# Reordering the last graph's projections: means directly behind the last v products, two q products two tiles later, and q gathers that wait for one tile

## The chip, the cores and the metric

The kernel runs on one core of a Trainium2 chip. The metric is the device time of one execution in microseconds (us), as the median of several runs of the same program. A single core runs here, so its time is the time of the kernel.

## The reference

Thirty-two graphs of 512 nodes with 512 features each share one sparse 0/1 adjacency matrix (density 0.0078, some 4 neighbours for each node). Each graph goes through two layers, everything in float32:

```python
# layer 0: masked attention, 8 heads of 64
h = relu(layernorm(x))
q, k, v = h @ Wq + bq, h @ Wk + bk, h @ Wv + bv      # split in heads
scores = q @ k.T / 8 + (1 - adj) * -1e9
x = x + softmax(scores) @ v @ Wo + bo
# layer 1: graph attention
h = relu(layernorm(x)) @ W
e = leaky_relu(h @ a1 [:, None] + h @ a2 [None, :]) * adj
x = x + elu(softmax(e) @ h + beta * h)
```

A node with no neighbour attends to all nodes alike in layer 0, so its result is the mean of all v. The kernel keeps these means as extra rows of the table of v.

## The kernel before

**Tiles and stages.** A graph has T = 4 tiles of 128 nodes; B = 32 graphs give 128 tiles. The nodes are permuted once so that each tile's edges fit 4 groups of 128 gathered rows. Two stages alternate:

- `stage_a(b)` makes the projections of graph b. For two tiles at a time, `turned_state` fetches x, normalises it and transposes it into `hT`; `keys_and_values` makes k and v of both tiles with seven half products (L872, a Strassen-like scheme) and stores them in the table `tab`; `queries` makes q (L42 with `wq,hT`), adds the bias on DVE (L804), copies in a column of the older graph (L807) and stores q in the table `qtab`. At the end come the means: `means` (L932) sums the v of the four tiles on TensorE, ACT scales them (L939), and four small SP stores (L943) put them into `tab`. All plain stores of these tables are issued by SP (`put`, L911).
- `stage_b(b)` does the edge work for each tile of graph b, and layer 1 for the same tile of graph b - LAG, with LAG = 2. POOL issues four kv gathers (L960; 128 rows with k and v of graph b and the layer-1 state of graph b - 2) and four q gathers (L983) for each tile. DVE multiplies and sums q times k (L1028, L1031), ACT takes the exponential and weighs v (L1037, L1042), and DVE makes the layer-1 weights of the edges (L1170). Then TensorE forms the edge sums (L1015, one bank `pd` for layer 1 and `px` for layer 0), transposes (L741) and runs the dense products with `wo` and `w` (L42). POOL also raises the variance to the power -0.5 in each norm (L761), fetches x for the residual (L774), and stores the output rows (L779, after L1238 on DVE).

The loop is `for b in range(B + LAG)`: stage_a(b + 1) while b + 1 < B, then stage_b(b). So graph 31's projections run beside the edge work of graphs 29 and 30, and no projections run after them. For the last two values of b only layer 1 is left; its gathers read smaller tables, `th`.

**Order.** The engines' programs are written out by a planner (`Plan.order`) before the launch. Every operation has an engine, an estimated duration, and a key, which is a due time in the planner's own units: tile n has the base `100 + 20 n`, S = 20 is one tile, and the projections of graph b start AHEAD = 6 tiles before its edge work. Among operations that can start at once on an engine, the one with the lowest key goes first; on TensorE a change of the matmul's form (128 rows or groups of 32) adds STAY = 1.0 to the key. An operation that is ready is never held back for its key alone: when nothing with a lower key can start within 0.2 us, it goes. Each engine then executes its list strictly in that order and waits where an input isn't there.

**Keys around the change** (in tiles; graph 31 begins at tile 124): the q products of its tiles 2 and 3 have 121.28 and 121.9, the last half product of v 121.74, the means 122 and 0.02 us. The edge sums of tile n have n + 1, the transposes n + 1.48, the product with `wo` n + 1.72, the layer-1 product n + 1.88. The gathers of tile n have n - 0.85 and n - 0.84.

**Buffers.** The gathered kv rows lie in a ring of 5 (`kv`), the gathered q rows in a ring of 2 (`qe`); each buffer holds two of the four groups of a tile. A kv buffer comes free with the edge sums of its tile.

**Waits.** A kv gather waits for everything that is written to `tab` of its graph: k, v and layer-1 state of four tiles and the means' rows. A q gather waits for everything that is written to `qtab` of its graph, thus for the q of all four tiles, though it reads rows of one tile only (and one zero row).

**Fillers.** `run_on` puts matmuls with no use for the result in front of some products of the last tiles: two matmuls behind the edge sums of the last five tiles of the edge work (L1078), and six in front of the edge sums of the first two tiles of graph 31 (L1183). They are always executed; the profile shows them as L42 with `wq` alone.

Of the kernel before, what the change touches and what calls it, by code (L numbers as in the profile page):

```python
# [64 lines left out]
class Plan:  # L65
# [14 lines left out]
    def buf(self, tag, name=""):  # L80
        return Buf(tag, name)
# [137 lines left out]
def kernel(  # L219
# [24 lines left out]
    B, N, D = x.shape  # L244
    T = N // P
# [20 lines left out]
    def wtile(shape, name, dt=F32):  # L266
        return work.tile(shape, dt, name=name, tag=name)

    def ring(n, shape, name):
        return [wtile(shape, f"{name}{i}") for i in range(n)]  # L270
# [3 lines left out]
        "hT": ring(3, [P, C, P], "hT"),  # L274
        "S": ring(3, [P, C // 2, P], "S"),
        "oT": ring(1, [P, C, P], "oT"),
# [37 lines left out]
    idx, qidx = wtile([P, T, NG], "idx", I32), wtile([P, T, NG], "qidx", I32)  # L314
# [11 lines left out]
    C_ = {n: buf(None, n) for n in (  # L326
        "wq", "wk", "wv", "wo", "w1", "rows", "c_row", "wa", "OH", "nzE", "idx", "qidx", "fin",
        "rmax", "dmax", "bad", "cap", "flag", "perm", "posi", "t1", "t2", "t3", "t4",
    )}
# [46 lines left out]
    def edges():  # L376
# [10 lines left out]
        def flat(b):  # L387
            return b.ap.rearrange("p a b -> p (a b)") if b.tag == "kv" else b.ap

        def f3(b, n, m):  # L390
            return flat(b)[:, : n * m].rearrange("p (n m) -> p n m", n=n)
# [194 lines left out]
        en = buf("w", "en")  # L586
        S = T * NG

        def enx():
            return flat(en)[:, : S * (MAXDEG + 3)].rearrange("p (t g m) -> p t g m", t=T, g=NG)  # L590

# [16 lines left out]
        def index():  # L608
            e = flat(en)[:, : S * (MAXDEG + 3)].rearrange("p (s m) -> p s m", s=S)
            m = flat(sc)  # L610
            kk, fi, no = m[:, 0:S], m[:, 32 : 32 + S], m[:, 64 : 64 + S]
            eq = f3(val, S, MAXDEG)

# [96 lines left out]


    S = 20.0
    AHEAD = 6

    def base(n):
        return 100.0 + n * S
# [18 lines left out]
    def dense(p, lhs, w):  # L735
        for c in range(C):
            product(nc, p, lhs[:, c, :], w[:, c, :], start=c == 0, stop=c == C - 1)
# [61 lines left out]
    def queries(b, t, key, hT):  # L799
        s = st[b]  # L800
        p, q = buf("D", "pq"), buf("q", f"q{b}_{t}")
        o = op("PE", 3.43, key, lambda: dense(p.ap, hT.ap, wq), r=[hT, C_["wq"]], w=[p])
        plan.reserve(o, q)
        op("DVE", 0.7, key, lambda: nc.vector.tensor_tensor(q.ap[:, 0:D], p.ap, bq_r, op=ALU.add), r=[p, C_["rows"]], w=[(q, "q")])  # L804
        if b >= LAG:
            s1 = st[b - LAG]["s1"]
            op("DVE", 0.1, key, lambda: nc.vector.tensor_copy(q.ap[:, D : D + 1], s1.ap[:, t : t + 1]),  # L807
               r=[(s1, t)], w=[(q, "s1")])
        put(b, lambda: s["qtab"].ap, t, lambda: q.ap, key, q, [(s["qtab"], t)])
# [98 lines left out]
    def put(b, dst, t, src, key, part, w):  # L908

        if b:  # L910
            op("SP", 0.1, key, lambda: nc.sync.dma_start(dst()[ts(t, P)], src()), r=[part], w=w, dma=P * D * 4)  # L911
        else:
            op("POOL", 1.3, key, lambda: nc.gpsimd.indirect_dma_start(
                dst()[:N], bass.IndirectOffsetOnAxis(ap=posi[:, t : t + 1], axis=0), src(), None,
                bounds_check=N - 1, oob_is_err=False), r=[part, C_["posi"]], w=w, dma=P * D * 4)

    def stage_a(b):
        s = st[b]
        s["qtab"] = buf("qtab", f"qtab{b}")
        mv, vs = buf("mv0", f"mv0_{b}"), []  # L920
        for t in range(0, T, 2):
            keys = [base(T * b + u - AHEAD) if b else 2.0 + 0.4 * S * u for u in (t, t + 1)]
            hT = [turned_state(b, u, key, mv) for u, key in zip((t, t + 1), keys)]
            vs += keys_and_values(b, t, keys[1], *hT) if b else plain_keys_and_values(t, keys, hT)
            for u in range(2):
                queries(b, t + u, keys[1] + (0.28, 0.9)[u] * S if b else keys[u] + 0.56 * S, hT[u])
        key = base(T * b + T - AHEAD) + 0.02 if b else keys[1] + S
        pv, vm = buf("D", "pvm"), buf("v", f"vm{b}")

        def means():  # L930
            for t in range(T):
                nc.tensor.matmul(  # L932
                    pv.ap[ts(t, G), :].rearrange("p (h f) -> p h f", f=HD), one32, vs[t][1]()[:, :, 0:HD],
                    start=True, stop=True,
                )

        o = op("PE", 1.0, key, means, r=[b for b, _ in vs], w=[pv], form=4)
        plan.reserve(o, vm)
        op("ACT", 0.62, key, lambda: nc.scalar.activation(  # L939
            vm.ap[:, :, 0:HD], pv.ap.rearrange("p (h f) -> p h f", f=HD), AF.Copy, scale=float(G) / P), r=[pv], w=[vm])  # L940
        tab, cols = place(b, VO, H * VW)
        for t in range(DUMMY):
            op("SP", 0.1, key, lambda t=t: nc.sync.dma_start(  # L943
                cols()[N + t : N + t + 1],
                vm.ap[G * t : G * t + 1].rearrange("p h f -> p (h f)")),
               r=[vm], w=[(tab, ("m", t))], dma=2080)

    def stage_b(b):

        s = st[b] if b < B else None  # L950
        old = st[b - LAG] if b >= LAG else None
        if old is not None:
            old["dn"] = buf("dn", f"dn{b}")
        if s is not None:
            s["x1"], s["hx"] = [None] * T, [None] * T
            s["mv1"], s["s1"] = buf("mv1", f"mv1_{b}"), buf("s1", f"s1_{b}")
            s["rd"] = buf("rd", f"rd{b}")

        def gather(dst, tab, t, g):
            nc.gpsimd.indirect_dma_start(  # L960
                dst, None, tab.ap, bass.IndirectOffsetOnAxis(ap=idx[:, t, g : g + 1], axis=0),
                bounds_check=N + DUMMY - 1, oob_is_err=False,
            )

        for t in range(T):
            kb = base(T * b + t)
            slots = [buf("kv", f"kv{b}_{t}_{i}") for i in range(2 if s is not None else 1)]
            slots += slots[len(slots) - 1 :] * (2 - len(slots))
            held = [{n: buf(None, n) for n in ("K", "V", "H")} for _ in range(2)]
            of = {KO: "KVH", VO: "VH", HO: "H"}  # L970
            for g in range(NG):
                for tab, c0, c1 in st[b]["tab"]:
                    op("POOL", 1.3, kb - 0.85 * S + 0.1 * g, lambda slots=slots, g=g, t=t, tab=tab, c0=c0, c1=c1: gather(
                        row(slots, g, c0, c1 - c0), tab, t, g),
                       r=[tab, C_["idx"]],
                       w=[(slots[g // 2], (g, c0)), *((held[g // 2][n], (g % 2, "row")) for n in of[c0])],
                       dma=P * (c1 - c0) * 4)
            if s is not None:
                qs = [buf("qe", f"qe{b}_{t}_{i}") for i in range(2)]
                for q in qs:  # L980
                    q.q, q.s1 = buf(None, "q"), buf(None, "s1")
                for g in range(NG):
                    op("POOL", 1.3, kb - 0.84 * S + 0.1 * g, lambda q=qs[g // 2], g=g, t=t: nc.gpsimd.indirect_dma_start(  # L983
                        q.ap[:, g % 2, :], None, s["qtab"].ap,
                        bass.IndirectOffsetOnAxis(ap=qidx[:, t, g : g + 1], axis=0),
                        bounds_check=N, oob_is_err=False),
                       r=[s["qtab"], C_["qidx"]], w=[(x, g % 2) for x in (qs[g // 2], qs[g // 2].q, qs[g // 2].s1)],
                       dma=P * QW * 4)
            wvb = edge_weights(b - LAG, t, kb, slots, held, qs if s is not None else None) if old is not None else None
            pv = layer0(b, t, kb, slots, held, qs, old is not None) if s is not None else None  # L990
            if old is not None:
                layer1(b - LAG, t, kb, slots, held, wvb, pv)
                if t == T - 1:
                    op("DVE", 0.16, kb + 1.6 * S, lambda: nc.vector.tensor_tensor(
                        dmax, dmax, old["dn"].ap[:, 0:2, :], op=ALU.max), r=[old["dn"]], w=[C_["dmax"]])
        if s is not None:
            self_sums(b, base(T * b + 6))
# [278 lines left out]
    for b in range(B + LAG):  # L1276
        if b + 1 < B:
            stage_a(b + 1)
        stage_b(b)
# [211 lines left out]
```

## Time and profile before

| | |
|---|---|
| median of 3 runs | 2706.05 us (2705.66 to 2709.75) |
| the profiled execution | 2724.4 us, its span 2722.6 us |
| mean granted TensorE clock | 0.989 |
| TensorE (PE), busy | 2657.9 us, 98% of the span |
| DVE, busy | 2054.8 us, 75% |
| ACT, busy | 1931.4 us, 71% |
| POOL, busy | 1818.6 us, 67% |
| bytes moved | 790.08 MB, 290 GB/s on average |

How to read it: the page and the trace come from one profiled execution, 18 us longer than the median, so a difference is made against that execution and then taken off the median. PE is TensorE, PEld its weight loads, SPq the DMA queue that SyncE issues. PEclk is the granted clock in tenths of full speed. "x8" counts instructions, and each float32 matmul of the program shows as two. A bracket at the end of a line of the timeline is the idle time of the engine ahead of it and what ended it. "issue" is time in which the engine waited for nothing that the profile shows.

### The profile page before, as it was taken

Reading aid. Unit: us, or ns where it says so; the run is one execution under the profiler, and the core shown is the slowest. Engines: PE = TensorE matmul, PEld = TensorE weight load, DVE = VectorE, ACT = ScalarE, POOL = GpSimd, SP = SyncE. Lnnn points to the kernel's source line nnn. Section 1 sums busy time; section 2 is a strip of 40 time slices with the busy share of each in tenths; the row PEclk is TensorE's granted clock in tenths of the full one; section 3 lists DMA queues with packets and bytes.
Section 4 is the critical chain, followed back from the end, with each engine's and each line's share of the span. In section 5 each row is a group of like instructions: output and inputs, shape, how many; then the busy total and the mean of one; then the engine's idle time right before and its main releaser. Section 6 shows DMA issues by size and latency. Waiting matters only on the chain.

```text
span 2722.6 us, 39798 instructions
## 1 busy us (share of the span) xinstructions
PE 2657.9 (98%) x10248; PEld 1216.0 (45%) x10248; DVE 2054.8 (75%) x5209; ACT 1931.4 (71%) x6183; POOL 1818.6 (67%) x1710
## 2 busy tenths in 40 slices
PE   9999999999999999999999999999999999999986
PEld 4444444444444444444444444444444444444432
DVE  7767777777777777777777777777777777777674
ACT  1557777687776777777777777777777777777772
POOL 2776766667766766666766766766666766666673
PEclk9999999999999999999999999999999999999998
DMA  5988888889888888888888888988888988988883
GB/s 180 259 282 315 295 301 304 285 297 311 300 296 300 298 295 315 290 293 312 300 303 303 302 296 299 312 298 295 313 296 288 323 291 299 315 292 284 304 259 107
DMA packets 237457, 790.08 MB, mean 290 GB/s; under 512 B 34667, under 2 KB 34675, under 8 KB 237222
## 3 DMA queue, kind: packets, MB, share of 16 engines
q0 software_dynamic: 156736, 644.99, 70.4%
q1 hardware_dynamic: 80486, 142.48, 14.0%
q8 instruction: 83, 1.36, 0.2%
q14 instruction: 152, 1.25, 0.1%
HBM read 617.88 MB, written 169.46 MB: 289 GB/s over the span
## 4 chain that ended last, share of the span: by engine, by line
PE 88%; issue 3%; POOL 3%; DVE 2%; DMA 2%; ACT 1%; another core or an unknown queue 0%; POOLq 0%; SPq 0%; DVEq 0%; ACTq 0%
PE pd L42 46%; PE pd L872 26%; PE pd L741 6%; PE pd L1015 4%; PE px L1015 4%; POOL kv L960 1%; PE pd L932 1%; PE pd L1111 1%; DMA qe<-qtab,qidx 1%; POOL qe L983 1%; DMA x<-in_x_dram,perm 1%; POOL x L774 0%; ACT kv L1042 0%; DMA kv<-tkv,idx 0%
## 5 line engine op out<-in xcount | busy, mean ns | idle before, releaser
L1042 ACT ACTIVATE kv<-kv 128x64 f32<-128x64 f32 x4096 | 1012.0, 336 | 5.2
L983 POOL DMA_INDIRECT qe<-qtab,qidx x512 | 546.8, 1068 | 229.9 <-issue 123.2
L960 POOL DMA_INDIRECT kv<-tab,idx x480 | 513.0, 1069 | 180.6 <-issue 119.6
L42 PE MATMUL pd<-wq,hT 128*128 128x512 f32 x1024 | 466.4, 599 | 1.3 <-ACT hT L796 1.3
L42 PE MATMUL pd<-wo,oT 128*128 128x512 f32 x1032 | 464.5, 593 | 0.0
L42 PE MATMUL pd<-w,gT 128*128 128x512 f32 x992 | 446.4, 593 | 1.4 <-DVE gT L1221 1.4
L774 POOL DMA_INDIRECT x<-in_x_dram,perm x252 | 352.0, 1397 | 85.8 <-issue 46.4
L1028 DVE TENSOR_TENSOR qe<-qe,kv 128x1024 f32<-128x1024 f32 x256 | 312.6, 1222 | 41.2 <-DMA qe<-qtab,qidx 23.4
L1031 DVE TENSOR_REDUCE s<-qe 128x16 f32<-128x1024 f32 x256 | 310.9, 1216 | 0.1
L42 PEld LDWEIGHTS pd<-wq,hT 128*128 128x128 f32 x1024 | 196.1, 193 | 246.0 <-issue 243.2
L42 PEld LDWEIGHTS pd<-wo,oT 128*128 128x128 f32 x1032 | 194.8, 190 | 240.0 <-issue 222.4
L42 PEld LDWEIGHTS pd<-w,gT 128*128 128x128 f32 x992 | 188.1, 190 | 239.7 <-issue 231.2
L761 POOL TENSOR_TENSOR mv<-mv,mhalf 128x1 f32<-128x1 f32 x256 | 171.1, 669 | 174.7 <-DVE mv L758 150.7
L779 POOL DMA_INDIRECT out_dram<-w,perm x128 | 158.5, 1238 | 153.2 <-DVE w L1238 120.1
L872 PE MATMUL pd<-wk,hT 128*128 128x512 f32 x496 | 241.5, 611 | 4.0 <-ACT hT L796 3.4
L872 PE MATMUL pd<-wt,S 128*128 128x512 f32 x496 | 237.7, 602 | 3.8 <-DVE k L880 3.7
L872 PE MATMUL pd<-wv,S 128*128 128x512 f32 x496 | 235.2, 597 | 4.1 <-DVE mv L763 2.1
L1232 ACT ACTIVATE w<-pd,dn 128x512 f32<-128x512 f32 x128 | 87.7, 685 | 178.0 <-PE pd L42 163.6
L1091 DVE CUSTOM_DVE_ANT_0 w<-hx,wa_r 128x512 f32<-128x512 f32 x256 | 175.5, 686 | 9.3 <-ACT hx L768 8.6
L756 DVE BATCH_NORM_STATS2 st<-x 128x6 f32<-128x512 f32 x256 | 176.5, 689 | 3.0 <-DMA x<-in_x_dram 0.4
L1083 DVE TENSOR_TENSOR x<-pd,x 128x512 f32<-128x512 f32 x128 | 88.1, 688 | 119.8 <-PE pd L42 86.5
L741 PEld LDWEIGHTS pd<-ident,w 128*128 128x128 f32 x1152 | 133.5, 142 | 82.7 <-issue 46.8
(213 smaller groups left out, 3569.6 us busy)
## 6 DMA issues: line engine op xcount, KB each, us to landing
qtab<-q SPq DMA_DIRECT2D x124, 258.0 KB
tab<-hx SPq DMA_DIRECT2D x120, 260.0 KB
tab<-v SPq DMA_DIRECT2D x120, 260.0 KB
tab<-k SPq DMA_DIRECT2D x120, 256.0 KB
qe<-qtab,qidx POOLq DMA_INDIRECT x512
kv<-tab,idx POOLq DMA_INDIRECT x480
x<-in_x_dram,perm POOLq DMA_INDIRECT x252
th<-hx SPq DMA_DIRECT2D x8, 260.0 KB
```

The source lines that it names most:

```text
L42: nc.tensor.matmul(out, lhsT, rhs, start=start, stop=stop)
L741: nc.tensor.transpose(p[:, ts(c, P)], src[:, ts(c, P)], ident)
L756: nc.vector.bn_stats(s6.ap, src.ap)
L774: nc.gpsimd.indirect_dma_start(dst, None, rows, bass.IndirectOffsetOnAxis(ap=perm[:, t : t + 1], axis=0), **lim)
L872: nc.tensor.matmul(p.ap, lhs()[:, c, :], rhs[:, c, :], start=first and c == 0, stop=c == K2 - 1, skip_group_check=True)
L960: nc.gpsimd.indirect_dma_start(dst, None, tab.ap, bass.IndirectOffsetOnAxis(ap=idx[:, t, g : g + 1], axis=0), bounds_check=N + DUMMY - 1, ...
L983: op("POOL", 1.3, kb - 0.84 * S + 0.1 * g, lambda q=qs[g // 2], g=g, t=t: nc.gpsimd.indirect_dma_start(q.ap[:, g % 2, :], None, s["qtab"]. ...
L1015: nc.tensor.matmul(out(g), lhs(g), row(slots, g, c0, n), start=True, stop=True)
L1028: nc.vector.tensor_tensor(qe.ap[:, :, 0:D], qe.ap[:, :, 0:D], sl.ap[:, :, KO : KO + D], op=ALU.mult)
L1031: nc.vector.tensor_reduce(sb.ap, qe.ap[:, :, 0:D].rearrange("p n (h f) -> p n h f", f=HD), axis=AX.X, op=ALU.add)
L1042: nc.scalar.activation(p[:, h, 0:HD], p[:, h, 0:HD], AF.Copy, scale=p[:, h, HD : HD + 1])
L1091: nc.vector.tensor_tensor_reduce(scr.ap, hx.ap[:, 1 : D + 1], row, 1.0, 0.0, op0=ALU.mult, op1=ALU.add, accum_out=dst)
```

## The change

Three edits, all for the last graph, b = 31, and all in keys and dependences; the set of instructions stays the same.

1. The means' key becomes that of the last v product's pair plus 0.75 tiles, 121.75, right behind the last half product of v (121.74), where it was 122.
2. The q products of tiles 2 and 3 (with their DVE and SP operations, which have the same key) get keys two tiles later: 123.28 and 123.9.
3. A q gather of graph 31 waits for the q of its own tile alone. The other graphs' q gathers wait for all four tiles as before.

```diff
     S = 20.0
+    QL, ML = 2.0, 0.75
     AHEAD = 6
@@ stage_a
             for u in range(2):
-                queries(b, t + u, keys[1] + (0.28, 0.9)[u] * S if b else keys[u] + 0.56 * S, hT[u])
-        key = base(T * b + T - AHEAD) + 0.02 if b else keys[1] + S
+
+                late = QL * S if b == B - 1 and t else 0.0
+                queries(b, t + u, keys[1] + (0.28, 0.9)[u] * S + late if b else keys[u] + 0.56 * S, hT[u])
+        key = (base(T * b + T - AHEAD) + 0.02 if b < B - 1 else keys[1] + ML * S) if b else keys[1] + S
         pv, vm = buf("D", "pvm"), buf("v", f"vm{b}")
@@ stage_b, the q gather
-                       r=[s["qtab"], C_["qidx"]], w=[(x, g % 2) for x in (qs[g // 2], qs[g // 2].q, qs[g // 2].s1)],
+                       r=[(s["qtab"], t if b == B - 1 else None), C_["qidx"]], w=[(x, g % 2) for x in (qs[g // 2], qs[g // 2].q, qs[g // 2].s1)],
```

## The prediction

> **What bounds the kernel now.** I read the page's 40 slices first, then the waits of TensorE in the tail, then the timelines of TensorE and POOL there, and last the busy time in 4 us windows. I write (b,t) for tile t of graph b. The changed lines act on graph 31, whose projections run from 2482 to 2551 us.
>
> ```profile
> PE   9999999999999999999999999999999999999986
> PEclk9999999999999999999999999999999999999998
> DMA  5988888889888888888888888988888988988883
> ```
>
> TensorE is full until the last two slices (68 us each). There is nothing to win before them except by moving work. The waits of TensorE from 2550 us to the end (total, times, longest):
>
> ```profile
> PE pd L1015 <- DVE wv L1170: 7.5, 2, 5.8
> PE pd L42 <- DVE wv L1170: 7.0, 1, 7.0
> PE pd L741 <- DVE w L1066: 4.0, 6, 1.3
> PE pd L1130 <- DVE s L1091: 3.2, 1, 3.2
> ```
>
> The first and last rows are the edge sums of (31,1) and (31,2) coming too late. TensorE's timeline, with the q products of tiles 2 and 3, the edge sums of (30,1), the means, and the sums of (31,0), (31,1), (31,2):
>
> ```profile
> 2527.00 3.60 PE L42 MATMUL pd<-wq,hT 128*128 128x512 f32 x8
> ...
> 2545.05 3.60 PE L42 MATMUL pd<-wq,hT 128*128 128x512 f32 x8
> 2548.57 1.07 PE L1015 MATMUL pd<-kv,wv 128*32 128x512 f32 x8
> ...
> 2550.33 1.05 PE L932 MATMUL pd<-v,one 128*32 128x512 f32 x8
> ...
> 2590.28 1.06 PE L1015 MATMUL pd<-kv,wv 128*32 128x512 f32 x8
> ...
> 2607.68 2.01 PE L1015 MATMUL pd<-kv,wv 128*32 128x512 f32 x8 [1.66 <-DVE wv L1170]
> ...
> 2628.21 2.03 PE L1015 MATMUL pd<-kv,wv 128*32 128x512 f32 x8 [5.85 <-DVE wv L1170]
> ```
>
> To 2590 the sums wait for nothing: TensorE's own order sets them. From 2602.5 they wait for data. That data comes from POOL's gathers:
>
> ```profile
> 2547.74 1.78 POOL L779 DMA_INDIRECT out_dram<-w,perm  x1 [4.00 <-DVE w L1238]
> ...
> 2555.67 1.00 POOL L983 DMA_INDIRECT qe<-qtab,qidx  x1 [0.30 <-issue]
> 2558.10 0.99 POOL L960 DMA_INDIRECT kv<-tab,idx  x1 [1.43 <-issue]
> 2560.61 0.57 POOL L761 TENSOR_TENSOR mv<-mv,mhalf 128x1 f32<-128x1 f32 x1 [1.51 <-DVE mv L758]
> ```
>
> Counting gathers back from the last one, 2558.10 is the first kv gather of graph 31. It stood 1.43 us: its table was complete only with the means' four stores, whose issue ended at 2553.30. After 2569 POOL issues without a break until 2615. DMA shares in 4 us windows (the number ahead of GB/s):
>
> ```profile
> 2544.00:2548.00 4.00, 4.00 (x10) 1.71 (x9) 2.58 (x8) 3.36 (x9) 0.26 (x1) 1.00 0.73 286
> 2548.00:2552.00 4.00, 4.00 (x42) 1.19 (x40) 3.25 (x8) 0.80 (x4) 3.39 (x3) 1.00 0.36 132
> 2552.00:2556.00 4.00, 3.08 (x19) 1.82 (x16) 1.16 (x4) 4.00 (x16) 3.08 (x4) 1.00 0.88 169
> 2556.00:2560.00 4.00, 4.00 (x11) 1.83 (x10) 2.66 (x6) 3.25 (x10) 1.67 (x2) 1.00 0.99 332
> ```
>
> From 2556 to 2612 the share is 0.92 to 1.04 in every window, so the transfers are the limit there. Just before it, (0.27 + 0.64 + 0.12) x 4 = **4.1 us** of transfer time lie unused.
>
> **What the skill says.** The Trainium skill, "Perfetto Trace Analysis", What "DMA-bound" means: an issuing sequencer whose track is solid DMA slices is a bound of its own. The trace agrees for POOL, with issues of 1.0 us and 0.30 between. "DMA: Bandwidth & Descriptors", Issuing engines are not separate DMA queues: transfers of all engines share 16 engines; the shares near 1 from POOL and SP together fit. The same page, Anatomy of one DMA, puts about 2.0 us fixed on one transfer; here 4.8 us passed from the last means store to the gather it released, so I use 4.8. "TensorE: Matmul & The Clock Gate", Why this matters for your kernels: avoid idle gaps above about 3 us, or the clock halves. The trace agrees: after gaps of 3.17 and 1.66 the clock is 0.59, after 5.85 it is 0.53, and the gaps of 0.9 to 1.3 leave 1.00.
>
> **The change part by part.** No instruction is added or removed.
>
> *q products later.* Each moves 8 matmuls, DVE's eviction (L804, 0.69) and copy (L807, 0.15), and an SP store (0.32). To the next start the two take 2530.44 - 2527.00 = 3.44 and 2548.57 - 2545.05 = 3.52: **6.96 us** leave TensorE's full part. The stage's remaining products move up, too; their inputs are then 3.4 us nearer, which I cost at nothing because TensorE has other ready products there. On SP and DVE the cover is some 30 us: tile 2's gather starts at 2592, tile 3's at 2606.
>
> *Means ahead of the sums of (30,1).* 0.88 us of TensorE (2550.33 to 2551.21), an ACT copy (0.61), four SP stores (1.20). They need the last v additions on DVE; the layer-1 product of 3.4 us behind the last v product should hide these. So the means start near 2550.33 - 6.96 - 1.8 = 2541.6 and the sums of (30,1) near 2548.57 - 6.96 + 0.88 = 2542.5. The sums' weights were ready at 2531.7. Their two kv slots come free 6.1 us earlier.
>
> *Gathers.* POOL stood 4.00 us for L1238 of the tile whose product comes after one moved q only: 3.44 earlier. The 1.43 goes as well: stores ending near 2544.6 plus 4.8 give 2549.4, before POOL gets there. Sum 4.9, capped by the 4.1 us of free transfer time. The gathers of tile 0 no longer stand behind q of tile 3, otherwise late by design; that wait is taken away and none added. Behind each gather on POOL stand the power of the next norm (L761, then hx on ACT), a fetch and a store, so the 1.51 at 2560 stays. **Gathers: -4.1 us.**
>
> *Where the q products land.* The order is made by a planner that takes the lowest key among ready products, and any ready one in an idle stretch. I expect q in the first waits behind the sums of (30,1) and (30,2), which now show 0.86 and 1.29 idle: 6.96 - 2.15 = 4.8 comes back. Sums of (31,0): -6.96 + 4.8 = -2.15 us, at 2588.1; their data (2589.6 - 4.1) are there. If the q's fall to the data waits instead, nothing comes back; if in smaller waits, all 6.96 does.
>
> *The end.* Sums of (31,1): data at 2607.6 - 4.1 = 2603.5, TensorE free at 2602.5 - 2.15 = 2600.4: about 3.1 us of idle where 4.8 were. This is near the clock's limit. I take it that the clock holds: both edge sums then take 1.88 (as at 2575.94) where they took 3.66, **-1.8 us**. Unseen, this is bounded by -3.6 (the 5.85 gap's clock too) and +1 (a longer slow stretch). The next tile's second multiply stands on DVE behind L1070 of (31,1), so it follows. Everything after is a chain and moves rigidly. -4.1 - 1.8 = **-5.9 us**.
>
> That difference is from an execution of 2724.4 us (span 2722.6 and 1.8 around it), 18 us above the median of 2706.05. At least some of this is late: ACT stood 11.25 us to 2679.6 for something the trace calls only "remote", after all that moves. I take the difference off the median: **2700 us**.
>
> **The rivals.** (1) *The q products come back whole and the gathers hardly gain.* For: the planner fills any wait, and each wait is shorter than a product. Then only the 1.43 of the means is left, with up to 3.4 of the store: 2702 to 2705, within 0.2%. That the moves change no order is the end of this case (2706). (2) *All of it is gained*: 6.96 on TensorE, both clock drops gone (3.6), less idle: 2694 to 2696. Against: 4.1 us of free DMA. (3) *Slower: POOL's queue head.* The planner counts some 2.7 us from a store's issue to its landing, beside 4.8 measured. Just-in-time gathers behind means, q of tile 2 and q of tile 3 would each stand 2.1 us with powers, fetches and all later gathers behind: 6.3 against 1.43 now, or +4.9; the clock drops longer (+1) and 1 to 2 of fetch and hx follow: 2713. It decides once POOL's stalls exceed what it gets back, 4.9. Against: q of both tiles has some 30 us to spare.
>
> **How the numbers follow.** A measurement of this kernel can tell about 0.2%, 5.4 us. The main case with (2) is faster by more: 0.50 (0.37 and 0.13). Its value is close to the line, and (1), with the main case without its clock gain (2702), is 0.37 within 0.2%. (3) and other disorder of the queues have 0.13. The range reaches from 2692 (case 2, a little further) to 2710 (part of case 3), with about 0.15 left out. The main case alone spans 2697 to 2703.
>
> **What would show it.** Right: the means and the sums of (30,1) near 2542; q of tiles 2 and 3 behind those sums; no 1.43 before the first kv gather of graph 31, which starts near 2553; the DMA window at 2548 fuller than 0.36; the sums of (31,1) near 2603 at full clock, 1.06 and not 2.01. Wrong: POOL standing over 2 us before gathers of graph 31, the sums of (31,1) at 2607 or later, or these steps right and the last edge sums of graph 31 not earlier than 2641.6.

## The result and the profile after

The changed kernel is slower. Its median is 2720.02 us (2716.72 to 2722.33, 6 runs) beside 2708.32 us for the kernel before (2705.66 to 2709.97, 6 runs). The ratio is 1.0039, with a 95% interval of 1.0028 to 1.0050: +11 to +12 us, where 2700 us was predicted. In a later set (e14 below), on a chip where the kernel before took 2722.72 us, the ratio was 1.0046 (1.0030 to 1.0063).

The page of after, the three rows of slices (span 2714.9 us, profiled execution 2716.72 us):

```profile
PE   9999999999999999999999999999999999999887
PEclk9999999999999999999999999999999999999999
DMA  5988898888888888888988888988988988988884
```

They hardly tell the two kernels apart. The spans don't either: the span before is 7.7 us *longer*. Its times fit a chip of the slower kind (last section), though which chip it was is not known. So I compare the stretch between two marks that both traces have: the start of the `px` edge sums of (29,3), ahead of everything that moves, and of (31,3). It takes 133.5 us before (2508.97 to 2642.48) and **138.5** after (2501.99 to 2640.52).

Lines of after are shifted: by 1 at L741 to L804 (a power is L762, transposes L742), by 3 from L932 on (means L935, gathers L963 and L986, edge sums L1018), and stores by 1 (L912); in kernels with the repair below by one more. TensorE's timeline (start, length, instruction, idle time ahead of it and what ended it):

```profile
2534.08 1.07 PE L935 MATMUL pd<-v,one 128*32 128x512 f32 x8
2534.97 1.04 PE L1018 MATMUL pd<-kv,wv 128*32 128x512 f32 x8
...
2537.68 3.70 PE L42 MATMUL pd<-wq,hT 128*128 128x512 f32 x8
...
2542.53 3.60 PE L42 MATMUL pd<-wq,hT 128*128 128x512 f32 x8
...
2565.06 1.97 PE L742 MATMUL pd<-ident,w 128*128 128x128 f32 x8 [7.43 <-DVE w L1069]
2567.34 4.98 PE L42 MATMUL pd<-wo,oT 128*128 128x512 f32 x8 [0.31 <-ACT oT L1084]
...
2589.95 1.07 PE L1018 MATMUL pd<-kv,wv 128*32 128x512 f32 x8
...
2608.70 2.03 PE L1018 MATMUL pd<-kv,wv 128*32 128x512 f32 x8 [3.71 <-DVE wv L1173]
...
2626.71 1.16 PE L1018 MATMUL pd<-kv,wv 128*32 128x512 f32 x8 [2.85 <-DVE wv L1173]
```

The first four lines are the plan come true. Moved to the time scale of before (+6.98), the means are at 2541.06 and the sums of (30,1) at 2541.95; both late q products stand behind those sums. The fifth line was not in the plan: 7.43 us without work ahead of the transposes of (30,2), where before had 1.29:

```profile
2565.26 1.31 PE L741 MATMUL pd<-ident,w 128*128 128x128 f32 x8 [1.29 <-DVE w L1066]
```

TensorE's waits in after from 2550 us on (total, times, longest) put it first:

```profile
PE pd L742 <- DVE w L1069: 9.9, 3, 7.4
PE pd L1018 <- DVE wv L1173: 6.6, 2, 3.7
```

What DVE and ACT were doing, from their timelines:

```profile
2563.80 0.16 DVE L764 SCALAR_TENSOR_TENSOR mv<-mv 128x1 f32<-128x1 f32 x1 [11.27 <-POOL mv L762]
2564.00 0.82 ACT L769 ACTIVATE hx<-x,mv 128x512 f32<-128x512 f32 x1 [9.70 <-DVE mv L764]
```

Both stood for one power on POOL, a 0.59 us instruction. POOL's timeline shows where that was:

```profile
2546.09 0.99 POOL L963 DMA_INDIRECT kv<-tab,idx  x1 [0.30 <-issue]
2553.06 1.00 POOL L986 DMA_INDIRECT qe<-qtab,qidx  x1 [5.97 <-DVE mv L759]
2559.55 1.00 POOL L986 DMA_INDIRECT qe<-qtab,qidx  x1 [5.49 <-DMA qtab<-q]
2560.86 1.00 POOL L986 DMA_INDIRECT qe<-qtab,qidx  x1 [0.30 <-issue]
2562.16 1.00 POOL L986 DMA_INDIRECT qe<-qtab,qidx  x1 [0.30 <-issue]
2563.18 0.59 POOL L762 TENSOR_TENSOR mv<-mv,mhalf 128x1 f32<-128x1 f32 x1
```

The power stands behind the four q gathers of (31,0), and the first two of these stood 5.97 and 5.49 us. The second waits for a q store. SyncE's timeline, with the two late q stores in one line, and the waits of its queue in the stretch 2530 to 2650 show the other half:

```profile
2544.88 11.91 SPq L912 DMA_DIRECT2D qtab<-q  x2
```
```profile
SPq L912 <- DMA qe<-qtab,qidx: 11.2, 1, 11.2
```

The q store of tile 3 waits, for 11.2 us, for a *gather* from the same table. The program has the q store of tile 2, the first of the four gathers, the q store of tile 3, and the other three gathers, in this order. The store of tile 3 waits for the first gather, and the second gather waits for that store. The first gather's 5.97 us are probably a wait for the store of tile 2, issued at 2544.88: the trace names a DVE operation, but the wait is gone in the kernels below where the two share no table. The gathers read rows of tile 0 and the stores write rows of tiles 2 and 3, but the waits are for the table as a whole. The third edit tells the planner that a gather needs its own tile alone. It does not alter how the waits are made: every gather's source is all of `s["qtab"].ap`. So what the third edit is said to do, that a q gather of graph 31 waits for its own tile alone, holds for the plan and not for the chip. The planner was free to place a gather ahead of a store that the program's waits then hold back, and the other way round.

In 4 us windows (busy time of PE, PEld, DVE, ACT, POOL, then PEclk, DMA share, GB/s) the hold is a hole in everything, with the granted clock at half behind it:

```profile
2556.00:2560.00 4.00, 1.64 (x4) 0.38 (x2) 0.00 (x0) 0.00 (x0) 0.45 (x1) 0.96 0.17 66
2560.00:2564.00 4.00, 0.00 (x0) 0.00 (x0) 0.20 (x3) 0.00 (x1) 3.20 (x5) 0.50 0.45 139
2564.00:2568.00 4.00, 2.63 (x9) 2.07 (x10) 3.86 (x12) 4.00 (x15) 3.08 (x4) 0.50 0.73 219
```

The Trainium skill, "DMA: Bandwidth & Descriptors", Two DMAs through the same engine are not ordered, says that the engine that issues a dependent DMA has to wait for the first one's semaphore, and that the data has landed once this is complete. This explains why such a wait lasts as long as it does. The trace agrees: it puts the store's wait down to a gather's DMA (11.2 us) and the next gather's to the store's (5.49 us). That there is a wait at all between rows that the two do not share comes from the program, which names the whole table.

### The profile page after: what moved, and what is told of

It reads as the page before. It is cut to its first block, busy times and chain, and to the rows that moved or that the text cites. A ratio compares the mean times of both kernels' runs of the same rounds, so it can differ in the third digit from the quotient of the medians.

```text
span 2714.9 us, 39798 instructions
## 1 busy us (share of the span) xinstructions
PE 2655.5 (98%) x10248; PEld 1217.1 (45%) x10248; DVE 2055.0 (76%) x5209; ACT 1925.7 (71%) x6183; POOL 1832.0 (67%) x1710
## 5 line engine op out<-in xcount | busy, mean ns | idle before, releaser
L986 POOL DMA_INDIRECT qe<-qtab,qidx x512 | 557.6, 1089 | 229.9 <-issue 114.5
L963 POOL DMA_INDIRECT kv<-tab,idx x480 | 508.9, 1060 | 166.2 <-issue 110.7
L762 POOL TENSOR_TENSOR mv<-mv,mhalf 128x1 f32<-128x1 f32 x256 | 173.2, 678 | 181.2 <-DVE mv L759 162.2
L742 PEld LDWEIGHTS pd<-ident,w 128*128 128x128 f32 x1152 | 134.7, 142 | 81.4 <-issue 38.9
```

The source lines that it names most:

```text
L762: op("POOL", 0.75, key, lambda: nc.gpsimd.tensor_tensor(mv.ap[:, t, 2:3], mv.ap[:, t, 2:3], mhalf[:, 0:1], op=ALU.pow), w=[(mv, t)])
L963: nc.gpsimd.indirect_dma_start(dst, None, tab.ap, bass.IndirectOffsetOnAxis(ap=idx[:, t, g : g + 1], axis=0), bounds_check=N + DUMMY - 1, ...
```

## The experiments

**Theory A**: the mutual hold of q stores and q gathers, above, is the loss. The rivals that carry other letters in the expectations lay it on the moves or on the means of the repair. No run was made of the third edit alone on the shared table, because the planner then puts out the instructions of before in the same order on all five engines. This already says that the third edit has an effect only together with another.

To take the hold away without taking away a needed wait, the repair gives graph 31 four q tables of its own, one for each tile (own tables), with row numbers counted within the tile:

```diff
+        "qlast": [dram.tile([P + 1, QW], F32, ...) for i in range(T)],
-nc.sync.dma_start(dst()[ts(t, P)], src())
+nc.sync.dma_start(dst()[ts(t, P)] if own is None else own[:P], src())
-q.ap[:, g % 2, :], None, s["qtab"].ap, ... qidx[:, t, g : g + 1]
+q.ap[:, g % 2, :], None, rings["qlast"][t] if b == B - 1 else s["qtab"].ap, ... (qrel if b == B - 1 else qidx)[:, t, g : g + 1]
```

Its set-up is four copies of the zero row and `qrel = min(qidx - 128 t, 128)`. In e1_own_tables it is done at the start. In the other own-table kernels it comes in mid-run, between two planned operations. The own tables take away all three waits at once (5.97, 11.2 and 5.49 us in after), so what each of them costs by itself is not shown. The kernels of one set ran on one chip: e1 to e4; e5 to e8; e9 to e11; e12 to e14.

**First set: repair, and pairs of edits on the shared table.**

e1_own_tables, all three edits on own tables:

> The changed kernel, but graph 31's q lies in four tables of its own, one for each tile, so that a store and a gather of different tiles touch no common table. The order of the instructions on TensorE, ACT and POOL is that of the changed kernel; only waits between q stores and q gathers go (and 5 small DVE instructions and 4 stores of 2 KB are added in the first 60 us, priced at 0.5 us). Theory A, store and gather hold each other: in the changed kernel the q store of tile 3 waits until tile 0's first q gather has landed, and tile 0's second q gather waits for that store, since both name the whole table; POOL stands, the power of the norm (L762) stands behind it, DVE behind that, TensorE behind that (7.43 us). Then here the store waits for no gather, TensorE's 7.43 us wait is at most 1.5, and the time falls by 9 to 16 us against the changed kernel: 2704 to 2711, ratio to before 0.998 to 1.001. Theory B, the order itself: the q products put ahead of the transposes of (30,1) and other moved rows cost it; nothing changes but waits, so 2717 to 2722, ratio 1.003 to 1.005. Theory C, the early kv gathers fill the DMA queues so that the q store lands late: POOL's stall of 5.97 ahead of the first q gather stays in part; ratio 1.000 to 1.003.

e2_means_own, without the late q products (`QL = 0.0`):

> The first and third edit, without the second: means behind the last v product, each tile's q gather waiting in the plan for its own tile alone, all q products at their old keys. In its order tile 0's first q gather stands ahead of the q store of tile 3, so the two hold each other as in the changed kernel. Theory A: POOL stands some 4 to 8 us before tile 0's second q gather, 3 to 10 us slower than before (2711 to 2718, ratio 1.001 to 1.004), though no q product is late. Theory B, late q products do the harm: none is late here; 2704 to 2709, ratio 0.999 to 1.000.

e3_means_late_q, without the third edit (`r=[s["qtab"], C_["qidx"]]`):

> The first and second edit, without the third: means early, q of tiles 2 and 3 two tiles late, every q gather waiting for all four tiles in the plan. TensorE's order is that of the changed kernel up to the edge sums of (30,2); in its order all q stores stand ahead of every q gather, so no store waits for a gather. Theory A: no hold; POOL waits at most once, for the last q store (2 to 4 us); 2703 to 2711, ratio 0.998 to 1.001. Theory B: the q products stand where they stand in the changed kernel; 2716 to 2722, ratio 1.003 to 1.005.

e4_late_own, without the first edit (the means' key as before):

> The second and third edit, without the first: q of tiles 2 and 3 late, q gathers waiting in the plan for their own tile, means at their old key. In its order the q stores of tile 2 and of tile 3 both stand behind q gathers of tile 0, and later q gathers behind them: two holds in place of one. Theory A: worse than or like the changed kernel, 10 to 25 us above before (2718 to 2733, ratio 1.004 to 1.009). Theory B: like the changed kernel or less, ratio 1.002 to 1.005. Theory C: the kv gathers of graph 31 start later since the means are late, so less of a jam; ratio 0.999 to 1.002.

Measured: e1 2709.44 us, ratio 0.9997 (0.9989 to 1.0006). e2 2715.8 us, 1.0023 (1.0013 to 1.0033). e3 2712.82 us, 1.0006 (0.9998 to 1.0014). e4 2717.47 us, 1.0022 (1.0014 to 1.0030).

The own tables take the loss away while all moves stay, and of the 5.97 us ahead of the first q gather 0.30 are left, against Theory C. e2 loses without any late q product, and e3, with both moves and the wait for the whole table, loses nothing that shows. SyncE's waits in the traces follow: a q store waits for a q gather for 7.8 us in e2 and three times, up to 17.2 us, in e4, and in e3 never. A miss: I expected more of e4 for its two holds, at least 1.004. Its two long waits of TensorE, 5.44 and 5.35 us, are together longer than the 7.43 of after, so they don't explain why it loses less; that stays open. By its time alone e4 fits Theory B (1.002 to 1.005) and not A; against B speak e3 here and e8 below.

**Second set: the repair in mid-run, on the pairs that contain the third edit.** e5_before_again is the kernel before, for one more look at the end of the run:

> The kernel before once more, for a second profiled execution: the first was 16 us above the median of its runs. If that was late, as the waits for a remote releaser at 2668 to 2684 us suggest, the stretch from the last edge sums of graph 31 to the end is 70 to 76 us here, where it was 81.0. If it lay early, that stretch is again 80 to 82.

> As e1 (the changed kernel with graph 31's q in four tables, one for each tile), but the four small stores and the four small DVE instructions that prepare the tables stand in the middle of the run, where TensorE covers them, not in the start. Theory A with the working of the prediction (the holds gone, the rest of the moves gains 5.9): 2700 to 2706 beside 2710.5 of before, ratio 0.997 to 0.999. Rival: the moves gain nothing even without the holds, and e1's time was not the start's: 2707 to 2711, ratio 0.999 to 1.0005.

> First and third edit with tables of their own (as in e6), q products at their old keys. Against e2 only the waits between q stores and q gathers differ. Theory A: e2 was 6 us above before through one hold; without it 2706 to 2711, ratio 0.9985 to 1.0003. Rival, its order costs by itself: like e2, 1.0015 to 1.003.

> Second and third edit with tables of their own (as in e6), means at their old key. Against e4 only the waits between q stores and q gathers differ. Theory A: e4 was 6 us above before through two holds; without them 2702 to 2709, ratio 0.997 to 0.9997, and above e6 by what the early means bring, 0 to 2 us. Rival: its order costs by itself: 1.001 to 1.003.

Measured: e5, one run, 2724.29 us; the stretch behind the last marks took 77.6 us, neither of the two expected values, so it settles nothing. e6 2723.46 us, 0.9985 (0.9978 to 0.9992). e7, edits 1 and 3, 2724.2 us, 0.9987 (0.9975 to 0.9999). e8, edits 2 and 3, 2724.04 us, 0.9982 (0.9973 to 0.9990). The same edits gave 1.0023 (e2) and 1.0022 (e4) on the shared table, on another chip. The hold explains each pair as it does the whole. No kernel with the tables alone ran on this chip, so how much of the 0.0036 and 0.0040 is the tables' own is not shown here; where such a kernel ran, on two other chips, it showed no gain (e9, e13 below).

**Third set: each edit alone.**

> The third edit alone, on four real tables (one for each tile's q of the last graph, set up in mid-run): the order of the kernel before otherwise, means behind the sums of (30,1), no late q product. Theory A (a whole table makes its store and its gathers hold each other; with own tables the first two edits only fill in beside it): ratio 0.998 to 1.000 of before, no stall over 1 us ahead of a q gather of the last graph. Rival D (the gain of the variants with own tables comes from the tables alone, the first two edits bring nothing): 0.998 to 0.999, the same as with all three edits within the intervals. Rival E (the tables only repair what the first two edits break): 1.000 to 1.001.

> The first edit alone: the means of the last graph right behind its last v products; q products and the order of gathers as before. Theory A (the holds come from the third edit's order alone): no store of the last graph's q that waits for a gather of the same graph; ratio 0.998 to 1.000. Rival B (earlier means put a wait or a lower clock of their own into the stretch): 1.001 to 1.003.

> The second edit alone: two tiles' q products of the last graph later; the gathers of tile 0 still stand behind all four q stores. Theory A and the prediction's rival of q products that come late for their gathers agree that the gathers then wait for the last store: 1.001 to 1.004 with one stall of POOL ahead of the first q gather of the last graph of 4 to 10 us. If the planner simply places all four early as before: 0.999 to 1.001.

Measured: e9 2708.36 us, 0.9997 (0.9988 to 1.0006). e10 2712.79 us, 1.0013 (1.0006 to 1.0019). e11 2717.71 us, 1.0034 (1.0021 to 1.0047).

e11 came as expected, and is what the third edit was made against. The q gathers of (31,0) wait for the last late q store, in POOL's timeline. Later TensorE stands before the edge sums of (31,0) and runs them at half clock (2.05 us). The way from the first wait to the second was not followed:

```profile
2562.59 1.01 POOL L986 DMA_INDIRECT qe<-qtab,qidx  x1 [4.24 <-DMA qtab<-q]
```
```profile
2584.90 2.05 PE L1018 MATMUL pd<-kv,wv 128*32 128x512 f32 x8 [6.56 <-issue]
```

e10 is a miss for Theory A: no q store or gather holds another in its trace, and it still loses some 3.5 us, within the range of Rival B (1.001 to 1.003). Its (31,1) is 4.5 us earlier than before, counted from (29,3), and (31,3) is 2.7 later. In between, one power stands behind POOL's gathers (DVE L764 waits 4.73 us for it), and TensorE waits for the weights of (31,2):

```profile
2619.72 2.03 PE L1018 MATMUL pd<-kv,wv 128*32 128x512 f32 x8 [9.84 <-DVE wv L1173]
```

So a move that only frees gathers earlier may lose by the order that the planner then gives to POOL's queue. That the power behind the gathers is the cause here was not tried alone. Nor is it known why each of the two moves loses by itself (1.0013, 1.0034) while both together, on the shared table, lose nothing that shows (e3, 1.0006).

**Fourth set: repair, tables alone and the change itself on one chip.** By the sets before it, own tables gained on the second chip and not on the first and third. This set was to say whether the gain belongs to the edits, to the tables or to the chip.

> All three edits on own tables set up in mid-run, the same kernel as e6_own_tables_mid, beside the kernel after and the third edit alone on own tables on one chip. If the set-up at the start is what cost e1_own_tables its 3 us: ratio 0.998 to 0.999 again, some 0.001 under e13_own_only_tables_again. If the chip of a run makes that difference: within 0.0006 of e13_own_only_tables_again, wherever both lie.

> The third edit alone on own tables, the same kernel as e9_own_only_tables. If the first two edits bring the gain that the holds covered: ratio 0.9993 to 1.0005 and e12_own_tables_mid_again 0.001 lower. If the tables alone bring it (rival D): the same ratio as e12_own_tables_mid_again.

> The changed kernel itself on the chip of the two before: ratio 1.003 to 1.005 if its loss doesn't hang on the chip; e12_own_tables_mid_again should be 0.004 to 0.0055 below it by Theory A.

Measured: e12 2720.62 us, 0.9993 (0.9984 to 1.0002). e13 2722.84 us, 0.9999 (0.9989 to 1.0009). e14 2734.83 us, 1.0046 (1.0030 to 1.0063). Taking the hold away, e14 to e12, is worth 2734.83 - 2720.62 = **14.2 us**, and 7.6 to 21.5 us by the outer ends of the two intervals. The ratios differ by 0.0053, within the 0.004 to 0.0055 expected. The tables alone bring nothing that shows (e9, e13). Whether the first two edits on own tables bring something is not settled by the times: e12 is 0.0006 below e13, with intervals that overlap; e6 is clear of 1; e1 is not. Nor is it settled whether the place of the set-up or the chip makes e1 and e6 differ.

The traces are steadier than the times. Time from the sums of (29,3) to those of each tile, less the same time before, in us:

| kernel | (30,1) | (30,2) | (30,3) | (31,0) | (31,1) | (31,2) | (31,3) |
|---|---|---|---|---|---|---|---|
| after | -6.7 | -2.1 | +6.7 | +6.7 | +8.2 | +4.7 | +5.0 |
| e14, after again | -6.6 | -1.8 | +6.3 | +6.2 | +8.0 | +4.9 | +5.5 |
| e6, repaired | -6.4 | -1.9 | -2.9 | -3.0 | -2.1 | -5.0 | -4.4 |
| e12, repaired again | -6.3 | -1.8 | -2.8 | -2.8 | -2.2 | -5.4 | -4.5 |
| e13, tables alone | -0.6 | -0.7 | -0.4 | -0.1 | -0.3 | -0.4 | +0.2 |

Up to (30,2) the change and its repair go alike. Between (30,2) and (30,3) the change loses 8.8 us. Of these, 6.1 are the longer wait of the transposes (7.43 for 1.29), 0.7 their clock (1.97 for 1.31), 1.4 the `wo` product's (4.98 for 3.60). The repaired kernel has no such step. In POOL's timeline of e12 the same four gathers, now from own tables, and the power follow one another:

```profile
2554.88 1.01 POOL L987 DMA_INDIRECT qe<-qlast,qrel  x1 [0.30 <-DVE q L809]
2556.19 1.04 POOL L987 DMA_INDIRECT qe<-qlast,qrel  x1 [0.30 <-issue]
2557.88 1.00 POOL L987 DMA_INDIRECT qe<-qlast,qrel  x1 [0.65 <-issue]
2559.18 1.00 POOL L987 DMA_INDIRECT qe<-qlast,qrel  x1 [0.30 <-issue]
2560.21 0.58 POOL L763 TENSOR_TENSOR mv<-mv,mhalf 128x1 f32<-128x1 f32 x1
```

The 5.97 in front of the first gather is gone too, so it came with the shared table as well, whatever the trace calls its releaser (0.30 us here). In e14 that first wait is 2.42 and the second 6.72, and TensorE's is 7.00.

One thing stays open: the marks of after and e14 show +5.0 and +5.5 us, the timed runs +11.7 and +12.1. The low ends of the two intervals are 7.6 and 8.2 us, so some 2 us or more of the loss lie outside the stretch or outside what single profiles show. The spans of e14 and e12, on one chip, differ by 13.3 us: 10.0 lie in the stretch and 3.5 ahead of it, where no planned operation was moved.

## Why the prediction was wrong

**The step that failed** is in *Gathers*: "The gathers of tile 0 no longer stand behind q of tile 3, otherwise late by design; that wait is taken away and none added." The edit took a dependence from the planner's list. In the program it only turned one wait round: the first gather of tile 0 no longer stands behind the store of tile 3, but that store now stands behind the gather (11.2 us on SyncE's queue), and the other three gathers still stand behind the store (5.49 us on POOL). The price is in the table: 8.8 us in one tile, 14.2 us in time against the same edits with real tables. The prediction took the words of the edit for a wait in the chip and did not ask which addresses the gather names. Its "some 30 us to spare" counts to each moved tile's own gather; in the shared table the gathers of tile 0 came first.

**The means and the q products.** *Means ahead of the sums of (30,1)* held: 2541.06 and 2541.95 on the scale of before, for 2541.6 and 2542.5. *Where the q products land*: both landed behind the sums of (30,1), one tile earlier than stated for the second. The size came out: -2.15 predicted at (31,0), -2.8 and -3.0 in the repaired kernels, which have the moves without the hold.

**The size of the gathers' gain.** Where the hold is absent, this term can be seen by itself. It was to be -4.1 us at (31,1), capped by free transfer time. The repaired kernels show -2.1 and -2.2 there, and -5.0 and -5.4 only one tile later, when the long wait before (31,2) shrinks. At the last edge sums they show -4.4 and -4.5 for -5.9. e1 shows -5.8, but its time doesn't.

**The end.** *I take it that the clock holds* was wrong for after, where the two edge sums of (31,1) took 3.70 us behind a wait of 3.71, and right in one of three kernels with all edits and own tables. With the hold gone the wait there came near the 3.1 us of the working, but in e12 the clock fell all the same: the first sums took 1.16 us, the second 1.75 and the fillers behind them 2.08 (1.12 at full clock), 4.6 in all where before had 4.7:

```profile
2606.49 1.16 PE L1019 MATMUL pd<-kv,wv 128*32 128x512 f32 x8 [3.36 <-DVE kv L1172]
2607.38 1.75 PE L1019 MATMUL px<-kv,OH 128*32 128x260 f32 x16
2609.05 2.08 PE L42 MATMUL pd<-wq 128*128 128x512 f32 x2
```

In e6, behind the same 3.36, the first sums took 2.03. In e1, behind 3.35, the clock held: both took 1.16.

**The rivals.** *Slower: POOL's queue head* named the place: gathers of graph 31 standing, with powers behind, decisive once POOL's stalls exceed 4.9 us. They came to 11.5. Its mechanism was close but not the same: it had stores that land 2.1 us late for each just-in-time gather. Here the two gathers stood 5.97 and 5.49 us, the second behind a store that the first had held. This case and other disorder of the queues had been given 13 of 100. What the prediction named as a sign of being wrong, POOL standing over 2 us before gathers of graph 31, is what the trace shows.

**The base.** Of the 18 us by which the profiled execution lay above the median, "at least some of this is late" was right in part: beside the trace of after, 7 us lay ahead of the sums of (29,3), and about 6 behind those of (31,3).

**A reading.** The last row of the table of waits in the prediction (L1130, 3.2 us) is not an edge sum but the transpose of `s` that TensorE runs just ahead of the edge sums of (31,1). The sum built on it, 4.8 us of idle there, is right.

## What to carry to other kernels

A dependence in a planner and a wait on the chip are two things: before pricing a wait as removed, look at which addresses each side of it names, and give the parts separate tables if they are to be separate. When a planner is told of fewer dependences than the program enforces, it can interleave a table's stores and gathers, and then look in the trace for a store that waits for a gather. Work that shares an in-order queue with such a gather, here a 0.59 us power, pays the hold in full.

## What was not expected of the hardware

- The chips differ by 12 to 20 us on this kernel (medians before of 2708 to 2711 us on some and 2723 to 2729 us on two others), and the difference has a place. The sums of (29,3) start at 2499.6 to 2507.4 us on the first kind and 2508.3 to 2515.2 on the second. The stretch from the sums of (31,3) to the end takes 71.6 to 75.6 us and 77.6 to 81.4. In between they agree: counted from (29,3), the marks of e5, e9 and e13, which all have the order of before, lie within 1.3 us of those of before, though e9 ran on the first kind and e5 and e13 on the second. These runs don't tell chip and time of measurement apart. Profiles of this kernel from different chips could be compared by stretches, not by spans.
- Nearly the same wait before the edge sums of (31,1) was followed by three clocks. After 3.35 us the clock held in e1 (both sums 1.16 us). After 3.36 us it was at half from the first sums in e6 (2.03), and in e12 it fell only during the second (1.16, then 1.75). Near that length the wait alone did not tell what the clock did.
